# Six edits to a four-layer image kernel: folds moved, small stores from another queue, held pieces spread, a power on POOL, planes in row pairs, two rows swapped

## The chip, the cores and the metric

The kernel runs on one core of one Trainium2 chip. The metric is the device time of one execution in microseconds (us), from the first to the last instruction, as the median of several executions. Engines are called as the profile calls them: PE (TensorE), DVE (VectorE), ACT (ScalarE), POOL (GpSimd) and SP (SyncE); PEld is PE loading weights.

## The reference

The input is an image of 256 by 256 tokens with 128 channels in fp32. Four layers follow one another, each with a group norm in front and a residual around it. Shortened:

```python
x = x + attention(gn(x))      # layer norm, row attention with 4 heads, gate
x = x + gated_product(gn(x))  # a, b = sigmoid((x@W1+b1)*(x@W2+b2)); z = einsum('bikc,bkjc->bijc', a, b), 16 channels
                              # out = sigmoid(x@Wg+bg) * (layernorm(z) @ Wz + bz)
x = x + normalised_product(gn(x))
x = x + shifted_conv(gn(x))   # a 9-tap convolution to one channel, shifts, two 1x1 products

def normalised_product(z):    # 128 channels
    zn = (z - mean(z)) * rsqrt(var(z) + 1e-5)       # over the channels, for each token
    a = sigmoid(zn @ Wga + bga) * (zn @ Wla + bla)
    b = sigmoid(zn @ Wgb + bgb) * (zn @ Wlb + blb)
    k = einsum('bimc,bmjc->bijc', a, b)             # 128 products of 256x256 planes
    return sigmoid(zn @ Wgo + bgo) * (layernorm(k) @ Wlo + blo)
```

The factor `rsqrt(var(z) + 1e-5)` is one number per token, 65536 in all.

## The kernel before

Channels lie on the 128 partitions, tokens along the columns. A *piece* is 2048 tokens (1 MB), and there are 32. The kernel is a chain of passes over the pieces; between two passes everything waits for a statistic or for data that the pass before has stored. In order: load, transpose and statistics; variance of the first layer norm; attention; gate projections; 16 plane products and their normalisation; gated update of x; normalised projections; 128 plane products; output pass; tap sums and image; last pass.

The normalised projections make the factor once in four pieces, in one tile of 128x512 (16 of its 128 rows are live). When the block's turn comes, its rows are spread over the partitions by matmuls and multiplied in:

```python
        def sums5(b):                 # after the second piece of a block of four: the sums for the next block
            ...                       # 32 matmuls into st: mean and mean square
            nc.scalar.activation(mean2, st[:, 0, :], AF.Square, bias=off2)
            nc.vector.tensor_tensor(var, st[:, 1, :], mean2, ALU.subtract)
            nc.vector.tensor_scalar(var, var, 0.0, None, ALU.max)
            nc.scalar.activation(var, var, AF.Sqrt, bias=epst)
            nc.vector.reciprocal(rs2[b], var)

        def normalise5(s):
            rb = broadcast_rows(psX, rs2[s // KB], s, "p5_rb")     # 4 matmuls
            ...                       # zn = (x - mean) * rb on DVE
```

Small results, 32 rows of four times 512 tokens per piece, go to memory by one store from ACT's queue, in the gate projections and in the tap sums:

```python
    def store_groups(dst, s, src):
        nc.scalar.dma_start(dst[:, s * SC : (s + 1) * SC].rearrange("c (q t) -> q c t", q=4), src)
```

A product of two planes reads rows p and p + 128 into partition p, so each packet is one row of 256 numbers, 1 KB (by the packet records of before, 95697 packets of 1024 bytes from 2684 to 2999 us):

```python
            A = sb.tile([P, 8, N], F32, name="p6_A")
            nc.sync.dma_start(A, aD[4 * q : 4 * q + 4, :].rearrange("c (t p n) -> p (c t) n", p=P, n=N))
```

Of the kernel before, what the change touches and what calls it, by code (L numbers as in the profile page):

```python
# [8 lines left out]
F32 = mybir.dt.float32  # L9
AF = mybir.ActivationFunctionType  # L10
# [20 lines left out]
def kernel(ctx: ExitStack, tc: tile.TileContext, a: dict, out: bass.AP):  # L31
# [104 lines left out]
    def store_groups(dst, s, src):  # L136

        nc.scalar.dma_start(dst[:, s * SC : (s + 1) * SC].rearrange("c (q t) -> q c t", q=4), src)
# [48 lines left out]
    with tc.tile_pool(name="f0", bufs=1) as sb, tc.tile_pool(name="f0ps", bufs=1, space=PSUM) as ps:  # L187
        cen = sb.tile([P, P], F32, name="f0_c")
        nc.vector.tensor_scalar(cen, ident, -1.0 / D, None, ALU.add)
        wa = sb.tile([P, 4 * D + NH], F32, name="f0_a")  # L190
        nc.vector.tensor_scalar(wa, w0, ln_w, None, ALU.mult)
        wb = sb.tile([P, 4 * D + NH], F32, name="f0_b")
        nc.vector.tensor_scalar(wb, w0, ln_b, None, ALU.mult)
        for lo, hi in ((0, 4 * D), (4 * D, 4 * D + NH)):
            pc = ps.tile([P, hi - lo], F32, name="f0_pc", tag=f"f0_pc{lo}")
            nc.tensor.matmul(pc, lhsT=cen, rhs=wa[:, lo:hi], start=True, stop=True)
            nc.vector.tensor_copy(w0c[:, lo:hi], pc)
        pq = ps.tile([P, 3], F32, name="f0_pq")
        for j, i in enumerate((0, 1, 3)):
            nc.tensor.matmul(pq[:, j : j + 1], lhsT=w0[:, i * D : (i + 1) * D], rhs=ln_b, start=True, stop=True)  # L200
        nc.vector.tensor_copy(cqkg, pq)
        pv = ps.tile([P, D], F32, name="f0_pv")
        nc.tensor.matmul(pv, lhsT=ones, rhs=wb[:, 2 * D : 3 * D], start=True, stop=True)
        for k in range(4):
            nc.vector.tensor_copy(cv[:, k, :], pv)

        w2c_ = const.tile([P, 6, D], F32, name="w2c_")
        wa2 = sb.tile([P, 6, D], F32, name="f0_a2")
        nc.vector.tensor_scalar(wa2[:, 0:5, :], w2[:, 0:5, :], lniw, None, ALU.mult)
        nc.vector.tensor_scalar(wa2[:, 5, :], w2[:, 5, :], lnow, None, ALU.mult)  # L210
        for lo, hi in ((0, 4), (4, 6)):
            pc = ps.tile([P, (hi - lo) * D], F32, name="f0_pc2", tag=f"f0_pc2{lo}")
            nc.tensor.matmul(
                pc, lhsT=cen, rhs=wa2[:, lo:hi, :].rearrange("p w d -> p (w d)"), start=True, stop=True
            )
            nc.vector.tensor_copy(w2c_[:, lo:hi, :].rearrange("p w d -> p (w d)"), pc)
        pb2 = ps.tile([P, 6], F32, name="f0_pb2")
        for i in range(6):
            nc.tensor.matmul(
                pb2[:, i : i + 1], lhsT=w2[:, i, :], rhs=lnib if i < 5 else lnob, start=True, stop=True  # L220
            )
        nc.vector.tensor_tensor(b2w, b2w, pb2, ALU.add)
        pt_ = ps.tile([P, NH], F32, name="f0_pt")
        nc.tensor.matmul(pt_, lhsT=ones, rhs=wb[:, 4 * D :], start=True, stop=True)
        nc.vector.tensor_copy(ctri, pt_)

    RES = NSC // 2 + 2
    with tc.tile_pool(name="x0", bufs=1) as xres, tc.tile_pool(name="p0", bufs=3) as sb:
        held = {s: xres.tile([P, SC], F32, name=f"x0_{s}") for s in range(RES, NSC)}
        with tc.tile_pool(name="p0ps", bufs=6, space=PSUM) as ps:  # L230
            for s in range(NSC):
# [12 lines left out]
                if s not in held:  # L244
                    nc.sync.dma_start(xT[:, s * SC : (s + 1) * SC], xc)

# [409 lines left out]
    with tc.tile_pool(name="x1", bufs=1) as xres, tc.tile_pool(name="xs1", bufs=3) as xsb:  # L656
        held = {s: xres.tile([P, SC], F32, name=f"x1_{s}") for s in range(R1)}
        with tc.tile_pool(name="p3", bufs=3) as sb, tc.tile_pool(name="p3ps", bufs=3, space=PSUM) as ps:
            for s in range(NSC):
# [15 lines left out]
                nc.scalar.activation(ab, s1, AF.Sigmoid)  # L675
                store_groups(abD, s, ab)


        order = sorted(range(NSC), key=lambda s: (s + 0.5) / R1 if s < R1 else (s - R1 + 0.4) / (NSC - R1))
        loaded = {}  # L680

# [653 lines left out]
```

## Time and profile before

Before: 4266.16 us, median of 3 runs (4259.32 to 4276.3), clock 0.879. The passes in the trace of before, each counted from one characteristic instruction to the next:

| stretch | us |
|---|---|
| start to the attention's first product | 341.4 |
| attention, to the first sigmoid of the gate projections | 1254.9 |
| gate projections and 16 plane products, to the last store of the normalised z issued | 224.9 |
| gated update, to the first sums of the normalised projections | 266.3 |
| normalised projections, to the first plane product | 596.1 |
| 128 plane products, to the first row broadcast of the output pass | 326.4 |
| output pass, to the first tap sum | 384.1 |
| tap sums and image, to the last pass's first fetch of the image | 210.7 |
| last pass | 661.3 |

The page's busy line, and its chain that ended last (followed back from the last instruction, by engine, then by line):

```profile
PE 3274.0 (77%) x20256; PEld 1706.4 (40%) x20256; DVE 2567.3 (60%) x2581; ACT 1965.5 (46%) x2290; POOL 1769.1 (41%) x752
...
PE 28%; DMA 8%; POOL 5%; DVE 4%; issue 3%; ACT 1%; POOLq 0%; SPq 0%; DVEq 0%; ACTq 0%
```

No engine is busy all the time, and the followed chain names PE for only 28%. POOL, with 5%, is seldom what others wait for.

### The profile page before, as it was taken

The numbers are of one execution on the slowest core, as the hardware profiler recorded it, in microseconds if no ns is written. First come the engines' busy times: TensorE is split into PE (matmuls) and PEld (weight loads), VectorE is DVE, ScalarE is ACT, GpSimd is POOL, SyncE is SP. The second block draws the span as 40 slices with busy tenths as digits, with TensorE's granted clock in tenths as the row PEclk, the third lists the DMA queues.
The fourth block names the chain that finished last, engine by engine and source line by source line (L and its number), as shares of the span: only waits on it lengthen the run. The fifth ranks groups of instructions, "written<-read, shape, count | busy, mean of one in ns | idle before, by whom it ended". The sixth has DMA issues, their size and how long they took to land. (4 is left out here: it accounts for less than half of the span.)

```text
span 4266.2 us, 52074 instructions
## 1 busy us (share of the span) xinstructions
PE 3274.0 (77%) x20256; PEld 1706.4 (40%) x20256; DVE 2567.3 (60%) x2581; ACT 1965.5 (46%) x2290; POOL 1769.1 (41%) x752
## 2 busy tenths in 40 slices
PE   3568999999999975567799999899788631555555
PEld 3414555555555531322233333777333200333333
DVE  3526888888888861256544444455566422777775
ACT  2555777777777742222334343344455410333332
POOL 3005777777777740345300000455334200555554
PEclk8788999999999987777899999999899855777777
DMA  6882333333333337477645343999777575444543
GB/s 240 304 305 85 116 111 116 116 110 116 115 111 116 115 130 265 174 242 241 237 161 193 150 182 123 310 311 315 281 287 282 207 247 191 156 164 165 164 164 92
DMA packets 320535, 800.54 MB, mean 188 GB/s; under 512 B 21311, under 2 KB 205132, under 8 KB 265756
## 3 DMA queue, kind: packets, MB, share of 16 engines
q1 hardware_dynamic: 243756, 745.87, 49.5%
q10 hardware_dynamic: 74496, 50.33, 3.8%
q8 instruction: 162, 2.65, 0.3%
q0 software_dynamic: 2032, 0.95, 0.1%
q14 instruction: 89, 0.73, 0.0%
HBM read 503.47 MB, written 293.60 MB: 187 GB/s over the span
## 5 line engine op out<-in xcount | busy, mean ns | idle before, releaser
L459 DVE TENSOR_TENSOR p_e<-p_S,triT 128x1024 f32<-128x1024 f32 x512 | 609.4, 1212 | 144.9 <-PE p_S L449 144.9
L469 POOL TENSOR_TENSOR p_es<-p_e 128x1024 f32<-128x1024 f32 x256 | 603.2, 2367 | 124.0 <-issue 67.3
L467 ACT ACTIVATE p_e<-p_e,mbT 128x1024 f32<-128x1024 f32 x512 | 551.8, 1137 | 61.4 <-DVE p_e L459 59.7
L873 PE MATMUL p_pm<-p_zn,wf 128*128 128x512 f32 x1024 | 464.7, 610 | 22.0 <-ACT p_a L894 20.6
L434 PE MATMUL p_mm<-p_xn,wf 128*128 128x512 f32 x768 | 407.1, 614 | 8.1 <-POOL p_xn L407 8.1
L407 POOL TENSOR_TENSOR p_xn<-p_xn,p_rs 128x1024 f32<-128x1024 f32 x64 | 153.6, 2400 | 492.5 <-DMA p_rs<-rsD 299.8
L1153 PE MATMUL p_pt<-ident,p_v 128*128 128x128 f32 x512 | 116.3, 421 | 282.7 <-POOL p_v L1146 282.7
L1127 POOL TENSOR_TENSOR p_z<-p_z,p_e 128x2048 f32<-128x2048 f32 x32 | 144.3, 4509 | 437.0 <-DMA p_e<-imgD 232.1
L873 PEld LDWEIGHTS p_pm<-p_zn,wf 128*128 128x128 f32 x1024 | 188.8, 194 | 296.3 <-issue 193.4
L449 PE MATMUL p_S<-p_q,p_k 32*128 32x256 f32 x4096 | 296.1, 401 | 5.0 <-DVE p_e L459 5.0
L1133 PE MATMUL p_pm<-p_z,w2c 128*128 128x512 f32 x512 | 246.6, 637 | 64.9 <-POOL p_z L1127 61.8
L449 PEld LDWEIGHTS p_S<-p_q,p_k 32*128 32x128 f32 x4096 | 186.1, 184 | 161.6 <-PE p_mm L425 91.7
L918 POOL MEMSET p_k<- 128x512 f32 x1 | 0.5, 524 | 602.0 <-DMA bD<-p_b 602.0
L482 PE MATMUL p_o<-p_e,p_v 128*32 128x256 f32 x4096 | 247.6, 382 | 0.0
L1293 PE MATMUL tp_z<-p_B,tp_at 128*128 128x256 f32 x1024 | 232.0, 384 | 18.1 <-DMA p_B<-bD 17.9
L1007 POOL TENSOR_TENSOR p_x<-p_x,p_g 128x2048 f32<-128x2048 f32 x32 | 145.1, 4534 | 234.9 <-DVE p_g L1004 202.2
L1146 POOL TENSOR_TENSOR p_v<-p_v,p_x 128x2048 f32<-128x2048 f32 x32 | 196.7, 6147 | 97.6 <-DVE p_v L1144 78.5
L931 POOL TENSOR_TENSOR p_k<-p_k,p_sq 128x512 f32<-128x512 f32 x128 | 162.5, 1270 | 159.2 <-ACT p_sq L929 159.2
L1153 PEld LDWEIGHTS p_pt<-ident,p_v 128*128 128x128 f32 x512 | 104.2, 226 | 309.2 <-POOL p_v L1146 309.2
L1293 PEld LDWEIGHTS tp_z<-p_B,tp_at 128*128 128x128 f32 x1024 | 193.1, 191 | 49.6 <-DMA p_B<-bD 22.7
L1142 DVE TENSOR_TENSOR p_v<-p_r,p_z 128x2024 f32<-128x2024 f32 x32 | 153.9, 4810 | 64.8 <-ACT p_r L1134 64.8
L1157 ACT COPY p_o<-p_pt 128x512 f32<-128x512 f32 x64 | 37.5, 586 | 332.1 <-PE p_pt L1153 332.1
(318 smaller groups left out, 6205.0 us busy)
## 6 DMA issues: line engine op xcount, KB each, us to landing
p_x<-x2T SPq DMA_DIRECT2D x64, 1024.0 KB
p_x<-x1T SPq DMA_DIRECT2D x48, 1024.0 KB
p_x<-x3T SPq DMA_DIRECT2D x31, 1152.0 KB
p_x<-x3T SPq DMA_DIRECT2D x33, 1024.0 KB
p_x<-in_x_dram SPq DMA_DIRECT2D x32, 1024.0 KB
p_x<-xT SPq DMA_DIRECT2D x64, 512.0 KB
p_rs<-rsD SPq DMA_DIRECT2D x64, 512.0 KB
p_rb<-rzD SPq DMA_DIRECT2D x256, 128.0 KB
```

Source lines behind the costliest of these rows:

```text
L434: nc.tensor.matmul(pm, lhsT=w, rhs=t["xn"][:, cs_], start=True, stop=True)
L449: nc.tensor.matmul(Ss[h // 2][:, h % 2, u, :], lhsT=t["k"][hp, r * N + u * P : r * N + (u + 1) * P], rhs=t["q"][hp, r * N : (r + 1) * N], ...
L459: nc.vector.tensor_tensor(e[:, :, 2 * p : 2 * p + 2, :].rearrange("p u h n -> p h u n"), Ss[p], triT[:, 2 * p : 2 * p + 2, :, :], ALU.add,)
L467: nc.scalar.activation(e[:, u, :, :], e[:, u, :, :], AF.Exp, bias=mbT[:, u, i : i + 1])
L469: nc.gpsimd.tensor_tensor(es, e[:, 0, :, :], e[:, 1, :, :], ALU.add)
L482: nc.tensor.matmul(t["o"][hp, r % 2, :], lhsT=t["v"][:, r * 2 + u, hp], rhs=e[:, u, h, :], start=(u == 0), stop=(u == 1),)
L873: nc.tensor.matmul(pm[:, c, :], lhsT=wf2[:, i, :], rhs=zns[s][:, k * CK : (k + 1) * CK], start=True, stop=True)
L931: nc.gpsimd.tensor_tensor(k2, k2, sq, ALU.add)
L1133: nc.tensor.matmul(pm, lhsT=w2c, rhs=src[:, 2 * c : 2 * c + 2, :], start=True, stop=True)
L1146: nc.gpsimd.tensor_tensor(q, q, xt[:, 1:, :], ALU.add)
L1153: nc.tensor.transpose(pt[:, k, :], qf[:, b * P : (b + 1) * P], ident)
L1293: nc.tensor.matmul(pz[:, t, :], lhsT=at[:, u, t * P : (t + 1) * P], rhs=B[:, 2 * c + u, :], start=(u == 0), stop=(u == 1))
```

## The change

Its intent: take small costs out of eight stretches. The core of the diff, cut:

```diff
 # 1. folds of the layer norms' weights: moved from in front of the first pass to behind its statistics
 # 2. small stores: the queue is an argument, and both callers give nc.gpsimd
-        nc.scalar.dma_start(dst[:, s * SC : (s + 1) * SC].rearrange("c (q t) -> q c t", q=4), src)
+        queue.dma_start(dst[:, s * SC : (s + 1) * SC].rearrange("c (q t) -> q c t", q=4), src)
 # 3. every fourth piece held between the gate projections and the gated update; zn fetched two blocks ahead
-        held = {s: xres.tile([P, SC], F32, name=f"x1_{s}") for s in range(R1)}
+        held = {s: xres.tile([P, SC], F32, name=f"x1_{s}") for s in range(0, NSC, NSC // R1)}
-            for i, s in enumerate(order):
+            for s in range(NSC):
 # 4. the factor as a power on POOL
-            nc.vector.tensor_scalar(var, var, 0.0, None, ALU.max)
-            nc.scalar.activation(var, var, AF.Sqrt, bias=epst)
-            nc.vector.reciprocal(rs2[b], var)
+            nc.vector.tensor_scalar(var, var, 0.0, EPS, ALU.max, ALU.add)
+            nc.gpsimd.tensor_tensor(rs2[b], var, mhalf.to_broadcast([P, CK]), ALU.pow)
 # 5. planes in row pairs: partition p holds rows 2p and 2p+1, packets of 2 KB; the transposes read every second column
-            nc.sync.dma_start(A, aD[4 * q : 4 * q + 4, :].rearrange("c (t p n) -> p (c t) n", p=P, n=N))
+            nc.sync.dma_start(A, aD[4 * q : 4 * q + 4, :].rearrange("c (p t) -> p c t", p=P))
+    Ac = A[:, c, :].rearrange("p (t k u) -> p t u k", t=2, u=2)
-            nc.tensor.transpose(pa[:, u, t * P : (t + 1) * P], A[:, 2 * c + t, u * P : (u + 1) * P], ident)
+            nc.tensor.transpose(pa[:, u, t * P : (t + 1) * P], Ac[:, t, u, :], ident)
 # 6. output pass: the next piece's z rows before its k rows
-                    (normalise_z if h else normalise_k)(s + 1)
+                    (normalise_k if h else normalise_z)(s + 1)
 ... (the same layouts for B, K, zn and the factor of k; order and buffers of the gated update)
```

More of the change, by code (lines that the diff above doesn't have):

```diff
@@ L134, with store_groups @@
     b2 = column("L3_conv_b2")
-    def store_groups(dst, s, src):
-        nc.scalar.dma_start(dst[:, s * SC : (s + 1) * SC].rearrange("c (q t) -> q c t", q=4), src)
+    def store_groups(queue, dst, s, src):
+        queue.dma_start(dst[:, s * SC : (s + 1) * SC].rearrange("c (q t) -> q c t", q=4), src)
     def gn_finish(stats, name):
@@ L186 @@
     nc.vector.memset(slide[:, 31:32], 1.0 / D)
-    with tc.tile_pool(name="f0", bufs=1) as sb, tc.tile_pool(name="f0ps", bufs=1, space=PSUM) as ps:
-        cen = sb.tile([P, P], F32, name="f0_c")
-        nc.vector.tensor_scalar(cen, ident, -1.0 / D, None, ALU.add)
-        wa = sb.tile([P, 4 * D + NH], F32, name="f0_a")
-        nc.vector.tensor_scalar(wa, w0, ln_w, None, ALU.mult)
-        wb = sb.tile([P, 4 * D + NH], F32, name="f0_b")
-        nc.vector.tensor_scalar(wb, w0, ln_b, None, ALU.mult)
-        for lo, hi in ((0, 4 * D), (4 * D, 4 * D + NH)):
-            pc = ps.tile([P, hi - lo], F32, name="f0_pc", tag=f"f0_pc{lo}")
-            nc.tensor.matmul(pc, lhsT=cen, rhs=wa[:, lo:hi], start=True, stop=True)
-            nc.vector.tensor_copy(w0c[:, lo:hi], pc)
-        pq = ps.tile([P, 3], F32, name="f0_pq")
-        for j, i in enumerate((0, 1, 3)):
-            nc.tensor.matmul(pq[:, j : j + 1], lhsT=w0[:, i * D : (i + 1) * D], rhs=ln_b, start=True, stop=True)
-        nc.vector.tensor_copy(cqkg, pq)
-        pv = ps.tile([P, D], F32, name="f0_pv")
-        nc.tensor.matmul(pv, lhsT=ones, rhs=wb[:, 2 * D : 3 * D], start=True, stop=True)
-        for k in range(4):
-            nc.vector.tensor_copy(cv[:, k, :], pv)
-        w2c_ = const.tile([P, 6, D], F32, name="w2c_")
-        wa2 = sb.tile([P, 6, D], F32, name="f0_a2")
-        nc.vector.tensor_scalar(wa2[:, 0:5, :], w2[:, 0:5, :], lniw, None, ALU.mult)
-        nc.vector.tensor_scalar(wa2[:, 5, :], w2[:, 5, :], lnow, None, ALU.mult)
-        for lo, hi in ((0, 4), (4, 6)):
-            pc = ps.tile([P, (hi - lo) * D], F32, name="f0_pc2", tag=f"f0_pc2{lo}")
-            nc.tensor.matmul(
-                pc, lhsT=cen, rhs=wa2[:, lo:hi, :].rearrange("p w d -> p (w d)"), start=True, stop=True
-            )
-            nc.vector.tensor_copy(w2c_[:, lo:hi, :].rearrange("p w d -> p (w d)"), pc)
-        pb2 = ps.tile([P, 6], F32, name="f0_pb2")
-        for i in range(6):
-            nc.tensor.matmul(
-                pb2[:, i : i + 1], lhsT=w2[:, i, :], rhs=lnib if i < 5 else lnob, start=True, stop=True
-            )
-        nc.vector.tensor_tensor(b2w, b2w, pb2, ALU.add)
-        pt_ = ps.tile([P, NH], F32, name="f0_pt")
-        nc.tensor.matmul(pt_, lhsT=ones, rhs=wb[:, 4 * D :], start=True, stop=True)
-        nc.vector.tensor_copy(ctri, pt_)
     RES = NSC // 2 + 2
@@ L245 @@
                     nc.sync.dma_start(xT[:, s * SC : (s + 1) * SC], xc)
+        with tc.tile_pool(name="f0", bufs=1) as fsb, tc.tile_pool(name="f0ps", bufs=1, space=PSUM) as ps:
+            cen = fsb.tile([P, P], F32, name="f0_c")
+            nc.vector.tensor_scalar(cen, ident, -1.0 / D, None, ALU.add)
+            wa = fsb.tile([P, 4 * D + NH], F32, name="f0_a")
+            nc.vector.tensor_scalar(wa, w0, ln_w, None, ALU.mult)
+            wb = fsb.tile([P, 4 * D + NH], F32, name="f0_b")
+            nc.vector.tensor_scalar(wb, w0, ln_b, None, ALU.mult)
+            for lo, hi in ((0, 4 * D), (4 * D, 4 * D + NH)):
+                pc = ps.tile([P, hi - lo], F32, name="f0_pc", tag=f"f0_pc{lo}")
+                nc.tensor.matmul(pc, lhsT=cen, rhs=wa[:, lo:hi], start=True, stop=True)
+                nc.vector.tensor_copy(w0c[:, lo:hi], pc)
+            pq = ps.tile([P, 3], F32, name="f0_pq")
+            for j, i in enumerate((0, 1, 3)):
+                nc.tensor.matmul(pq[:, j : j + 1], lhsT=w0[:, i * D : (i + 1) * D], rhs=ln_b, start=True, stop=True)
+            nc.vector.tensor_copy(cqkg, pq)
+            pv = ps.tile([P, D], F32, name="f0_pv")
+            nc.tensor.matmul(pv, lhsT=ones, rhs=wb[:, 2 * D : 3 * D], start=True, stop=True)
+            for k in range(4):
+                nc.vector.tensor_copy(cv[:, k, :], pv)
+            w2c_ = const.tile([P, 6, D], F32, name="w2c_")
+            wa2 = fsb.tile([P, 6, D], F32, name="f0_a2")
+            nc.vector.tensor_scalar(wa2[:, 0:5, :], w2[:, 0:5, :], lniw, None, ALU.mult)
+            nc.vector.tensor_scalar(wa2[:, 5, :], w2[:, 5, :], lnow, None, ALU.mult)
+            for lo, hi in ((0, 4), (4, 6)):
+                pc = ps.tile([P, (hi - lo) * D], F32, name="f0_pc2", tag=f"f0_pc2{lo}")
+                nc.tensor.matmul(
+                    pc, lhsT=cen, rhs=wa2[:, lo:hi, :].rearrange("p w d -> p (w d)"), start=True, stop=True
+                )
+                nc.vector.tensor_copy(w2c_[:, lo:hi, :].rearrange("p w d -> p (w d)"), pc)
+            pb2 = ps.tile([P, 6], F32, name="f0_pb2")
+            for i in range(6):
+                nc.tensor.matmul(
+                    pb2[:, i : i + 1], lhsT=w2[:, i, :], rhs=lnib if i < 5 else lnob, start=True, stop=True
+                )
+            nc.vector.tensor_tensor(b2w, b2w, pb2, ALU.add)
+            pt_ = ps.tile([P, NH], F32, name="f0_pt")
+            nc.tensor.matmul(pt_, lhsT=ones, rhs=wb[:, 4 * D :], start=True, stop=True)
+            nc.vector.tensor_copy(ctri, pt_)
@@ L675 @@
                 nc.scalar.activation(ab, s1, AF.Sigmoid)
-                store_groups(abD, s, ab)
-        order = sorted(range(NSC), key=lambda s: (s + 0.5) / R1 if s < R1 else (s - R1 + 0.4) / (NSC - R1))
+                store_groups(nc.gpsimd, abD, s, ab)
         loaded = {}
         def fetch1(pool, tag, bufs):
-            for s in order:
+            for s in range(NSC):
                 if s not in held and s not in loaded:
@@ L697 @@
             for q in range(4):
-                A = sb.tile([P, 8, N], F32, name="z_A")
-                nc.sync.dma_start(A, abD[4 * q : 4 * q + 4, :].rearrange("c (t p n) -> p (c t) n", p=P, n=N))
-                B = sb.tile([P, 8, N], F32, name="z_B")
-                nc.sync.dma_start(B, abD[16 + 4 * q : 20 + 4 * q, :].rearrange("c (t p n) -> p (c t) n", p=P, n=N))
+                A = sb.tile([P, 4, 2 * N], F32, name="z_A")
+                nc.sync.dma_start(A, abD[4 * q : 4 * q + 4, :].rearrange("c (p t) -> p c t", p=P))
+                B = sb.tile([P, 4, 2 * N], F32, name="z_B")
+                nc.sync.dma_start(B, abD[16 + 4 * q : 20 + 4 * q, :].rearrange("c (p t) -> p c t", p=P))
                 for c in range(4):
@@ L729 @@
                 nc.sync.dma_start(
-                    znD[4 * q : 4 * q + 4, :].rearrange("c (t p n) -> p (c t) n", p=P, n=N),
-                    zq.rearrange("p c (t n) -> p (c t) n", t=2),
+                    znD[4 * q : 4 * q + 4, :].rearrange("c (p t) -> p c t", p=P),
+                    zq,
                 )
@@ L739, in fetch_zn @@
             def fetch_zn(b):
-                zns[b] = sb.tile([P, 4, CK], F32, name="p4_zn", bufs=4)
+                zns[b] = sb.tile([P, 4, CK], F32, name="p4_zn", bufs=3)
                 for c in range(4):
@@ L745, in fetch_zn, with finish @@
                     )
-            def finish(i, x2):
-                s = order[i]
+            def finish(s, x2):
                 for c in range(4):
@@ L753 @@
             pending = []
+            for b in range(2):
+                fetch_zn(b)
             for _ in range(4):
                 fetch1(sb, "xs2", 4)
-            for i, s in enumerate(order):
-                for b in (s // 4, order[min(i + 2, NSC - 1)] // 4):
-                    if b not in zns:
-                        fetch_zn(b)
+            for s in range(NSC):
+                if s % 4 == 1 and s // 4 + 2 < NSC // 4:
+                    fetch_zn(s // 4 + 2)
                 xt = held[s] if s in held else loaded[s]
@@ L783 @@
                 nc.gpsimd.tensor_tensor(xt, xt, gt, ALU.add)
-                pending.append((i, xt))
+                pending.append((s, xt))
                 if len(pending) > 1:
                     finish(*pending.pop(0))
-                    if order[i - 1] not in held:
+                    if s - 1 not in held:
                         fetch1(*((xsb, "xs", 3) if len(loaded) % 7 < 3 else (sb, "xs2", 4)))
@@ L825 @@
     KB = 4
+    mhalf = const.tile([P, 1], F32, name="mhalf")
+    nc.vector.memset(mhalf, -0.5)
     rs2 = [rs2_pool.tile([P, CK], F32, name=f"rs2_{b}") for b in range(NSC // KB)]
@@ L919 @@
         for q in range(D // 4):
-            A = sb.tile([P, 8, N], F32, name="p6_A")
-            nc.sync.dma_start(A, aD[4 * q : 4 * q + 4, :].rearrange("c (t p n) -> p (c t) n", p=P, n=N))
-            B = sb.tile([P, 8, N], F32, name="p6_B")
-            nc.sync.dma_start(B, bD[4 * q : 4 * q + 4, :].rearrange("c (t p n) -> p (c t) n", p=P, n=N))
-            K = sb.tile([P, 8, N], F32, name="p6_K")
+            A = sb.tile([P, 4, 2 * N], F32, name="p6_A")
+            nc.sync.dma_start(A, aD[4 * q : 4 * q + 4, :].rearrange("c (p t) -> p c t", p=P))
+            B = sb.tile([P, 4, 2 * N], F32, name="p6_B")
+            nc.sync.dma_start(B, bD[4 * q : 4 * q + 4, :].rearrange("c (p t) -> p c t", p=P))
+            K = sb.tile([P, 4, 2 * N], F32, name="p6_K")
             for c in range(4):
                 pz = tri_product(nc, ps, sb, A, B, c, ident, nc.vector.tensor_copy).rearrange("p t n -> p (t n)")
-                nc.scalar.copy(K[:, 2 * c : 2 * c + 2, :].rearrange("p t n -> p (t n)"), pz)
+                nc.scalar.copy(K[:, c, :], pz)
                 sq = sb.tile([P, 2 * N], F32, name="p6_sq")
@@ L931 @@
                 nc.gpsimd.tensor_tensor(k2, k2, sq, ALU.add)
-            nc.sync.dma_start(kD[4 * q : 4 * q + 4, :].rearrange("c (t p n) -> p (c t) n", p=P, n=N), K)
+            nc.sync.dma_start(kD[4 * q : 4 * q + 4, :].rearrange("c (p t) -> p c t", p=P), K)
         nc.vector.scalar_tensor_tensor(k1, k1, -1.0 / D, k1, ALU.mult, ALU.mult)
@@ L939 @@
         nc.sync.dma_start(
-            rkD.rearrange("o (t p n) -> p (o t) n", p=P, n=N), k1.rearrange("p (t n) -> p t n", n=N)
+            rkD.rearrange("o (p t) -> p (o t)", p=P), k1
         )
@@ L1037 @@
             nc.scalar.copy(st, pp)
-            store_groups(sD, s, st)
+            store_groups(nc.gpsimd, sD, s, st)
     with tc.tile_pool(name="img", bufs=1) as sb, tc.tile_pool(name="imgps", bufs=1, space=PSUM) as ps:
@@ L1282, in tri_product @@
 def tri_product(nc, ps, sb, A, B, c, ident, evacuate):
+    Ac = A[:, c, :].rearrange("p (t k u) -> p t u k", t=2, u=2)
+    Bc = B[:, c, :].rearrange("p (u n) -> p u n", u=2)
     pa = ps.tile([P, 2, N], F32, name="tp_a")
@@ L1293, in tri_product @@
             nc.tensor.matmul(
-                pz[:, t, :], lhsT=at[:, u, t * P : (t + 1) * P], rhs=B[:, 2 * c + u, :], start=(u == 0), stop=(u == 1)
+                pz[:, t, :], lhsT=at[:, u, t * P : (t + 1) * P], rhs=Bc[:, u, :], start=(u == 0), stop=(u == 1)
             )
```

## The prediction

> **What bounds the kernel now.** No single engine does: the page shows PE busy 77% of the span, DVE 60%, ACT 46%, POOL 41%. The kernel is a chain of some ten passes over the image, each ended by statistics, so I took it pass by pass. First the busy times by stretch, for five passes in turn: the two gate projections (1595 to 1755 us), the gated update of x (1845 to 2078), the 128 products of planes (2684 to 2999), one period of the output pass, the tap sums (3390 to 3557).
>
> ```profile
> core 0: us, PE busy (x) PEld busy (x) DVE busy (x) ACT busy (x) POOL busy (x), PEclk, DMA share, GB/s
> ...
> 3111.54:3122.64 11.10, 9.44 (x32) 3.50 (x33) 7.21 (x7) 6.30 (x7) 4.54 (x2) 1.00 0.75 284
> 1595.00:1755.00 160.00, 76.82 (x500) 16.74 (x492) 24.03 (x32) 42.11 (x64) 0.00 (x0) 0.73 0.67 252
> 1845.00:2078.00 233.00, 182.98 (x501) 68.83 (x500) 154.41 (x192) 67.98 (x62) 144.79 (x32) 0.83 0.74 234
> 3390.00:3557.00 167.00, 61.58 (x258) 7.04 (x258) 43.07 (x32) 18.73 (x32) 0.00 (x0) 0.51 0.69 248
> 2684.00:2999.00 315.00, 292.17 (x1536) 251.09 (x1535) 169.49 (x256) 139.33 (x257) 161.56 (x128) 0.99 0.99 312
> ```
>
> The products are at the DMA limit (share 0.99). The gate projections and tap sums have every engine under half busy and a DMA share near 0.68: something else paces them. Then the waits of the tap sums, the gated update and the output pass, one line from each answer (total us, times, longest):
>
> ```profile
> ACT p_st L1037 <- DMA sD<-p_st: 135.7, 29, 8.1
> ```
> ```profile
> PE p_pz L774 <- DMA p_zn<-znD: 74.2, 6, 35.8
> ```
> ```profile
> PE p_pm L982 <- DVE p_zn L976: 51.4, 31, 1.7
> ```
>
> The first is a wait for small stores, the second for a fetch that comes late, the third one wait of 1.66 us in each of 31 periods. Then the chain of waits in the normalised projections, where the factor is made once in four pieces:
>
> ```profile
> 2209.84 7.05 PE p_st L848 x64
> ...
> 2216.97 0.70 ACT p_m L854
> ...
> 2220.21 0.72 ACT p_var L858
> ...
> 2220.95 1.28 ACT L894
> ...
> 2222.25 1.12 ACT p_a L894
> ...
> 2223.41 5.23 PE p_pm L873 x8
> ```
>
> PE stands 2.94 us because ACT loads the square-root table, takes the root and loads the sigmoid table back; then it runs eight matmuls in 5.23 us instead of 3.70. Last the start: the first transposes begin only here, though the first piece had landed at 6.6 us by the landing records.
>
> ```profile
> 40.67 7.51 PEld L240 LDWEIGHTS p_t<-ident,p_x 128*128 128x128 f32 x48 [0.47 <-issue]
> ```
>
> [...] The small stores are written as [4, 32, 512] from 128 partitions[...]
>
> ```profile
> q10 hardware_dynamic: 74496, 50.33, 3.8%
> ```
>
> ACT's queue holds 32 output stores of 2048 packets and 64 small stores of 128: 73728. The remaining 768 are completions, and 32 x 16 + 64 x 4 is just 768.
> [...] The first zn fetches (16 partitions each) moved 104 GB/s from 1840 to 1850. [...]
> [...]
> [...]
>
> **The change, part by part.**
>
> *Folds behind the statistics.* The transposes can start at about 7 us instead of 40.7. The three preloaded pieces had landed by 14.6 us and DMA then idled until 45, so about 30 us of loading time is won, not 34, because this pass runs at a DMA share of 0.94 to 0.99. The folds' PE and DVE work (15 to 20 us and 36 to 40 us on the trace, 9 us together) moves onto the path between the last statistic and the factor; part overlaps the 3.6 us aggregate, so +8. I add +4 for folds' DVE operations that the scheduler may put early, where DVE then waits for weights that land at 14 to 37 us. Net -18.
>
> *Small stores from POOL's queue.* Per piece a busy engine carries 8 load packets of 8 KB (0.36 us in these passes) and, if one of the four, 32 store packets of 2 KB at 0.084 us: 2.9 + 2.7 = 5.6 us by estimate; the measured pieces take 163/32 = 5.1 us and 167/32 = 5.2 us. [...] Saved: 32 x 1.2 = 38, of which I book 36 for the gate projections; 32 x 1.3 = 42 [...] for the tap sums. Together -74.
>
> *Every fourth piece held.* Now pieces 0 to 7 are held and used throughout, so two of four zn buffers are pinned and each next block is fetched when it is needed: 74 us of PE wait, 36 of them before the first product and 38 later. With blocks in order and a fetch two blocks ahead the later ones vanish. What remains is DMA: per piece 224 packets of 8 KB x 0.39 / 16 = 5.5 and 64 zn packets x 0.225 / 16 = 0.9, 6.4 us x 32 = 203. The first zn fetch goes ahead of four loads of x, some 9 us earlier. From 1836 to about 2040 instead of 2078: -38, and I add -4 because packets should be shorter than 0.39 us without the bursts.
>
> *POOL power.* A period of four pieces takes 71.9 us: four pieces of 15.0, the sums 7.05, and 4.85 of gap. Without the root, its two tables and the 3.35 us reciprocal nearly all of the gap goes: 7 x 4.5 = -31. The power has some 20 us until its rows are used, except in block 0, where it is on the path: +6 if it takes 10 us (my guess). Net -25.
>
> *Planes in row pairs.* 96 MB in packets of 1 KB (0.052 us by the packet records) become 2 KB ones; the first pass shows 0.094 us for those. 49152 x 0.094 / 16 = 289 us against 319. PE alone needs 2.22 us per plane (6.67 per three when nothing waits), 285 us. So this goes from 320 to about 295: -25; the 16 planes of the gated layer give 1 more.
>
> *z before k in the output pass.* The next piece's z rows are ready half a piece sooner, and k has one more product's time. The 1.66 us wait goes: 11.1 to 9.5, checked against DMA (three transfers of 1 MB a piece are 384 packets of 8 KB: 384 x 0.345 / 16 = 8.3 us). 31 x 1.55 = 48; ACT's 4.4 us of moments may now delay a sigmoid, so I book -40.
>
> Sum: -18 - 74 - 42 - 25 - 26 - 40 = -225. The attention pass (1114 us and more) and the last pass (654 us) are untouched. 4266 - 225 = 4041, put at 4040.
>
> **Rivals.** (a) The power is slow. If POOL takes more than about 20 us for 128x512, PE waits in every block: at 40 us, 7 x 20 for the blocks and 30 more for block 0 are +170, so about 4210 in all. Nothing in the trace measures it; the long slack speaks against it, the missing figure for it. (b) The strided transposes load weights slower: 512 of 0.14 us, doubled +72 us, part hidden: near 4090. (c) The loads do not use what the stores set free: three buffers and a latency of some 8 us give 3.9 us per piece only if both overlap; if the pace stays at 4.5, 64 x 0.6 = +38: 4078. (d) Early-placed fold operations stall DVE until 37 us; the first part becomes +8: 4066. (e) Where DMA is freed, [...] packets lengthen; over the three DMA-heavy passes perhaps +30.
>
> **Range and chances.** The parts are mostly independent; an error of 10 to 15 us in each of six gives about 35. For 8 in 10: 3980 to 4115. Only (a) or two others together would spoil the 2% (85 us): faster 0.93, within 0.05, slower 0.02.
>
> **What would show it.** First transpose near 7 us; pieces of the gate projections and tap sums under 4.2 us; no wait for zn after the first; no table loads inside the normalised projections and a period near 67.3; the products at 2.3 us per plane with packets of 2 KB; periods of 9.5 us in the output pass. Wrong would be: pieces still at 5 us (then the four engines were not the limit), a wait for the power, transposes over 0.3 us, or the output pass waiting for DVE at another product.

- "The four" are DMA engines, as I read the records, which name none. In the trace of before a small store has 4 completions and an output store 16. While small stores moved data, at most four of their packets were under way in 90% of the time in the gate projections and 92% in the tap sums; of the output stores there were 12 or more in 93% of it.
- For the small stores, 1.2 and 1.3 us are the measured 5.1 and 5.2 us a piece less 3.9 us. The 3.9 was an estimate with nothing in the trace for how POOL's queue would spread the stores.
- For the tap sums 38 of the 42 us were booked; the 4 us taken off stood for an effect. So small stores come to -36 - 38 = -74, and the sum, with this term in it, to -225: 4266 - 225 = 4041, put at 4040. Without it, it would be -229.
- In rival (c), the latency of a load in the tap sums of before is 7.6 us (median of 32, from issue to first use).

## The result, and the profile after

After: 4576.12 us, median of 4 runs (4571.91 to 4585.05), against 4270.35 us for before beside it. The ratio is 1.0722, with a 95% interval of 1.0693 to 1.0751: 7% slower, where 5% faster was predicted.

The page after, with the lines that answer to those shown of before:

```profile
PE 3246.8 (71%) x20256; PEld 1710.5 (37%) x20256; DVE 2550.4 (56%) x2574; ACT 1937.9 (42%) x2268; POOL 2478.9 (54%) x824
...
PE 25%; POOL 19%; DMA 6%; DVE 3%; issue 2%; ACT 1%; POOLq 0%; SPq 0%; DVEq 0%; ACTq 0%
...
L858 POOL TENSOR_TENSOR rs<-p_var,mhalf 128x512 f32<-128x512 f32 x8 | 655.4, 81924 | 370.0 <-DVE p_var L857 370.0
```

POOL is busy 710 us longer than before, and its share of the chain rose from 5% to 19%. The last line gives most of it: the eight powers take 81,924 ns each, 655.4 us together. The line of waits shows who paid (total us, times, longest):

```profile
PE p_rb L814 <- POOL rs L858: 518.6, 8, 84.2
```

Eight waits, one per block. One period of the normalised projections, from the chain that ended last (start, length, what):

```profile
2119.92 7.05 PE p_st L848 x64
...
2126.99 0.70 ACT p_m L854
...
2129.02 81.94 POOL rs L858
...
2211.00 2.09 PE p_rb L814 x8
2213.09 14.70 PE p_pm L872 x32
```

(The profile counts two records for each of these matmul calls: x64 is 32 calls, x8 is 4.) As in the chain before, the sums take 7.05 us, and the table loads are gone as intended (15 of 1.28 us each in this pass before, one after). But the power then holds the chain for 82 us. PE still had products of the block before, whose last one ends at 2149.0 in the timeline, and then stood still until 2211.0: 62 us of the power's 82, so a slack of 20.

Now the other passes. The first transpose starts here (timeline, start and length):

```profile
6.28 3.28 PEld L200 LDWEIGHTS p_t<-ident,p_x 128*128 128x128 f32 x16 [6.28 <-issue]
```

And the busy times by stretch for the same five passes as in the prediction: gate projections, gated update, tap sums, plane products, one period of the output pass.

```profile
core 0: us, PE busy (x) PEld busy (x) DVE busy (x) ACT busy (x) POOL busy (x), PEclk, DMA share, GB/s
1570.00:1660.00 90.00, 59.56 (x468) 15.88 (x460) 22.47 (x30) 36.79 (x58) 18.75 (x28) 0.92 1.00 378
1770.00:1960.00 190.00, 158.85 (x456) 58.62 (x448) 137.70 (x172) 62.02 (x57) 129.84 (x29) 0.88 0.79 239
3735.00:3850.00 115.00, 54.89 (x232) 6.44 (x224) 38.85 (x29) 17.01 (x29) 26.70 (x30) 0.51 0.94 327
3096.00:3370.00 274.00, 262.52 (x1384) 232.67 (x1384) 152.80 (x232) 124.47 (x230) 147.00 (x116) 1.00 0.96 326
3425.34:3434.70 9.36, 9.36 (x33) 3.50 (x32) 7.14 (x8) 6.19 (x6) 4.55 (x1) 1.00 0.90 338
```

The gate projections and the tap sums now run at a DMA share of 1.00 and 0.94, where it was 0.67 and 0.69: their pacing limit is gone. The output pass has PE busy in the whole period. The same stretches as in the table of before, side by side:

| stretch | before | after | difference |
|---|---|---|---|
| start | 341.4 | 312.7 | -28.7 |
| attention | 1254.9 | 1255.6 | +0.7 |
| gate projections, 16 products | 224.9 | 175.6 | -49.3 |
| gated update | 266.3 | 244.6 | -21.7 |
| normalised projections | 596.1 | 1091.1 | +495.0 |
| 128 products | 326.4 | 318.3 | -8.1 |
| output pass | 384.1 | 331.8 | -52.3 |
| tap sums, image | 210.7 | 175.2 | -35.5 |
| last pass | 661.3 | 670.0 | +8.7 |
| sum | 4266.2 | 4575.0 | +308.8 |

Of the signs that the prediction named, the first transpose (6.3 us), the paces, the missing table loads, the waits for zn and the output pass came as said. The products came to 2.36 us a plane (274 us for 116) and not 2.3, the period near 67.3 us did not come, and a wait for the power is on its list of what would be wrong.

So the traces say that five of the edits together save 196 us, one costs 495, and the last pass, which no edit touches, is 9 us longer. My theory is that the power's duration, and nothing around it, is the loss. The rivals: POOL's place is the trouble (any work there, or the stores on its queue, delay others); the power has a large start-up and would be cheap in another shape; or the loss needs two of the edits together.

### The profile page after: what moved, and what is told of

Same layout as the page of the kernel before. It is cut to its first block, busy times and chain, and to the rows that moved or that the text cites. A ratio compares the mean times of both kernels' runs of the same rounds, so it can differ in the third digit from the quotient of the medians.

```text
span 4575.0 us, 52129 instructions
## 1 busy us (share of the span) xinstructions
PE 3246.8 (71%) x20256; PEld 1710.5 (37%) x20256; DVE 2550.4 (56%) x2574; ACT 1937.9 (42%) x2268; POOL 2478.9 (54%) x824
## 3 DMA queue, kind: packets, MB, share of 16 engines
q0 software_dynamic: 19440, 17.83, 1.4%
## 4 chain that ended last, share of the span: by engine, by line
PE 25%; POOL 19%; DMA 6%; DVE 3%; issue 2%; ACT 1%; POOLq 0%; SPq 0%; DVEq 0%; ACTq 0%
POOL rs L858 14%; PE p_pm L872 7%; PE p_pm L981 5%; POOL p_v L1145 4%; PE tp_z L1294 3%; PE p_pm L1132 3%; PE p_pt L1152 3%; DMA p_B<-bD 2%; DVE p_v L1141 2%; PE p_st L848 1%; DMA p_x<-x3T 1%; DMA sD<-p_st 1%; PE tp_a L1288 1%; PE p_rz L814 1%; PE p_rb L814 1%
## 5 line engine op out<-in xcount | busy, mean ns | idle before, releaser
L858 POOL TENSOR_TENSOR rs<-p_var,mhalf 128x512 f32<-128x512 f32 x8 | 655.4, 81924 | 370.0 <-DVE p_var L857 370.0
L814 PE MATMUL p_rb<-rs,sel 32*128 32x512 f32 x256 | 44.1, 763 | 518.6 <-POOL rs L858 518.6
L865 DVE SCALAR_TENSOR_TENSOR p_zn<-p_x,gn_mean,p_rb 128x1024 f32<-128x1024 f32 x64 | 78.9, 1274 | 523.9 <-PE p_rb L814 523.9
L893 ACT ACTIVATE p_a<-p_pm,b2w 128x1024 f32<-128x1024 f32 x64 | 71.3, 1114 | 660.4 <-PE p_pm L872 660.4
```

Of the source, the lines that this page charges most:

```text
L858: nc.gpsimd.tensor_tensor(rs2[b], var, mhalf.to_broadcast([P, CK]), ALU.pow)
```

## The experiments

Twelve kernels ran, in three groups; each group shared its runs of before (medians 4267.06, 4265.91 and 4265.99 us).

**The power undone.** All other edits stay.

```diff
-            nc.vector.tensor_scalar(var, var, 0.0, EPS, ALU.max, ALU.add)
-            nc.gpsimd.tensor_tensor(rs2[b], var, mhalf.to_broadcast([P, CK]), ALU.pow)
+            nc.vector.tensor_scalar(var, var, 0.0, None, ALU.max)
+            nc.scalar.activation(var, var, AF.Sqrt, bias=epst)
+            nc.vector.reciprocal(rs2[b], var)
```

> The kernel after with only the factor of the normalised projections taken as before (square root on ACT, reciprocal on DVE); everything else of the change stays. My theory: the power on POOL is the whole reason for the loss. Between the starts of the normalised projections and of the plane products the trace has 596.1 us before and 1091.1 after, 495 more, and no other edit falls into that stretch; so this kernel should take 4576 - 495 = 4081 us, range 4060 to 4100, that is 0.956 of the kernel before, and the eight waits of PE for the factor should be gone. Rival: POOL's stores, or the other order of things, also cost time that the power hides; then it stays above 4120. Second rival: the gains of the other parts came only because something else was late; then it is near 4266.

Measured: 4082.36 us (4077.06 to 4089.21, 5 runs), ratio 0.9573 [0.956, 0.9586]. The normalised projections take 597.9 us, as before. Undoing the power alone gives back 494 us.

**The power alone.** The kernel before with that one edit.

> The kernel before with the power on POOL as its only change. Theory (the power costs the same with or without the other edits, since none of them falls into its stretch): the normalised projections grow by 495 us as in the kernel after, 4267 + 495 = 4762, range 4735 to 4785, ratio 1.116. Rival (the loss needs another edit beside it, such as the stores on POOL's queue): clearly less than 4700.

Measured: 4763.34 us (4759.68 to 4765.91, 4 runs), ratio 1.1167 [1.1149, 1.1184]. The loss, 497 us, is the same without the other edits, so it needs no partner.

**The power on half of the columns** (wrong result: the other half is only copied).

```diff
-            nc.gpsimd.tensor_tensor(rs2[b], var, mhalf.to_broadcast([P, CK]), ALU.pow)
+            hc = CK // 2
+            nc.gpsimd.tensor_tensor(rs2[b][:, :hc], var[:, :hc], mhalf.to_broadcast([P, hc]), ALU.pow)
+            nc.gpsimd.tensor_copy(rs2[b][:, hc:], var[:, hc:])
```

> The kernel after with the power on half of the columns (256 of 512) and a copy for the others: wrong result on purpose, to read the cost law. Theory (cost per column of 128 values, 81.9 / 512 = 0.16 us, and a slack of 20 us): one power takes 41 us, PE waits 21 us in seven blocks and 41 in block 0, 188 us in all instead of 516; total 4576 - 328 = 4248, range 4225 to 4275. Rival (most of the 82 us is fixed, a start-up of the operation): over 4400. Rival (the copy or the wrong values change other stages): the difference does not lie in the normalised projections.

Measured: 4254.53 us (4252.37 to 4257.83, 4 runs), ratio 0.9973 [0.9958, 0.9988]. One power took 41.1 us, and the line of PE's wait for the factor is now this (block 0 is left out of the window):

```profile
PE p_rb L814 <- POOL rs L860: 151.2, 7, 21.6
```

That is 151.2 / 7 = 21.6 us per block, which is the power's 41.1 us less about 20 us of slack. The law "wait = duration less slack" holds at two points.

**The power by itself.** Ten POOL operations behind the last pass, on squared weights.

```diff
+        for i, (pp, n) in enumerate(((128, 512), (128, 256), (128, 128), (128, 64), (128, 16), (16, 512), (64, 512))):
+            r = sb.tile([P, CK], F32, name=f"m_r{i}")
+            nc.gpsimd.tensor_tensor(r[:pp, :n], v[:pp, :n], mhalf[:pp].to_broadcast([pp, n]), ALU.pow)
+        ...  # exponent 2; base 1 everywhere; a plain product
```

> The cost of the power by itself: the kernel with Newton's method in place of the power, with ten POOL operations added behind the last pass: powers of 128x512, 128x256, 128x128, 128x64, 128x16, 64x512 and 16x512 with exponent -0.5, 128x512 with exponent 2, 128x512 with base 1 everywhere, and a product of 128x512. Theory (per column and side by side over the partitions): 82, 41, 20.5, 10.2, 2.6 us for the first five; the same 82 us for 64 and 16 partitions; 82 us whatever base and exponent; 1.3 us for the product. Rival: a fixed part, then 128x16 takes far more than 2.6 us; rival: time goes with the number of values, then 16x512 takes about 10 us; rival: it depends on the values, then exponent 2 or base 1 is short. The total says nothing here, since the operations stand at the end.

Measured (one run, correct); from the groups by form, with busy us and mean ns:

```profile
L1183 POOL TENSOR_TENSOR m_one<-ones,mhalf 128x512 f32<-128x512 f32 x1 | 82.4, 82400 | 9.6 <-DMA out_dram<-p_o 9.6
L1179 POOL TENSOR_TENSOR m_r<-m_v,mhalf 128x512 f32<-128x512 f32 x1 | 81.9, 81918 | 0.0
L1179 POOL TENSOR_TENSOR m_r<-m_v,mhalf 16x512 f32<-16x512 f32 x1 | 81.9, 81915 | 0.0
...
L1181 POOL TENSOR_TENSOR m_sq<-m_v,m_two 128x512 f32<-128x512 f32 x1 | 81.9, 81905 | 0.0
...
L1179 POOL TENSOR_TENSOR m_r<-m_v,mhalf 128x16 f32<-128x16 f32 x1 | 2.9, 2885 | 0.0
L1185 POOL TENSOR_TENSOR m_mul<-m_v 128x512 f32<-128x512 f32 x1 | 1.0, 1029 | 0.0
```

From 16 to 512 columns it is (81,918 - 2,885) / 496 = 159 ns a column, with a fixed part of about 0.3 us. It does not matter how many partitions are used (16, 64 or 128), and the two exponents and the two sets of bases that were tried make no difference beyond 0.5 us. The product of the same tile with itself takes 1.03 us, one eightieth.

**The same factor from plain POOL operations.** One DVE operation on the bits gives a first guess, and three rounds of Newton's method follow.

```diff
-            nc.gpsimd.tensor_tensor(rs2[b], var, mhalf.to_broadcast([P, CK]), ALU.pow)
+            y = rs2[b]
+            t = sb.tile([P, CK], F32, name="p5_t", bufs=1)
+            nc.vector.tensor_scalar(y.bitcast(I32), var.bitcast(I32), -0.5, 1597463007.0, ALU.mult, ALU.add)
+            for _ in range(3):
+                nc.gpsimd.tensor_tensor(t, y, y, ALU.mult)
+                nc.gpsimd.tensor_tensor(t, t, var, ALU.mult)
+                nc.gpsimd.tensor_scalar(t, t, -0.5, 1.5, ALU.mult, ALU.add)
+                nc.gpsimd.tensor_tensor(y, y, t, ALU.mult)
```

> The kernel after with the power written as twelve plain POOL operations: one DVE operation on the bit pattern gives a first guess of the inverse root, then three rounds of Newton's method of three products and one scale-and-add each. From the trace POOL takes 1.27 us for a product of 128x512, so 9 x 1.27 + 3 x about 0.8 = 14 us, inside the slack of 20 us that PE had between the start of the power (2129.0) and its last product before the wait (2149.0). Theory (it is the time of this operation and not its place on POOL that costs): no wait for the factor in blocks 1 to 7, a period of 131.05 - 62.05 = 69.0 us, block 0 pays 14 us instead of 82; 7 x 62.05 + 68 = 502 us less than 4576, so 4074, range 4050 to 4095. Rival (POOL's work of whatever kind stands in the way of DVE here, or its semaphores come late): waits of PE for POOL remain, and it stays above 4120.

Measured: correct, 4062.4 us (4055.08 to 4064.61, 5 runs), ratio 0.9516 [0.9503, 0.9529]. One round, and the use of the factor, in the timeline:

```profile
2130.32 1.04 POOL L865 TENSOR_TENSOR p_t<-rs 128x512 f32<-128x512 f32 x1 [53.74 <-DVE rs L861]
2131.43 1.27 POOL L866 TENSOR_TENSOR p_t<-p_t,p_var 128x512 f32<-128x512 f32 x1
2132.79 0.62 POOL L867 TENSOR_SCALAR p_t<-p_t 128x512 f32<-128x512 f32 x1
2133.50 1.27 POOL L868 TENSOR_TENSOR rs<-rs,p_t 128x512 f32<-128x512 f32 x1
```

The twelve operations end at 2143.8, and PE takes the factor at 2149.6 without a wait; in the whole stretch PE waits for POOL once, 16.2 us in block 0. The period is 67.2 us, against 72.1 with the root on ACT and about 131 with the power. So POOL was a good place, and the idea of the edit (no table loads, work in the slack) was worth its gain; only the operation was wrong.

**The same on DVE, spread.** Nine operations, two behind each product's evacuation.

```diff
+            for _ in range(3):
+                todo.append(lambda: nc.vector.scalar_tensor_tensor(t, y, -0.5, y, ALU.mult, ALU.mult))
+                todo.append(lambda: nc.vector.tensor_tensor(t, t, var, ALU.mult))
+                todo.append(lambda: nc.vector.scalar_tensor_tensor(y, t, 1.5, y, ALU.add, ALU.mult))
 ...
+                    root5(2)         # takes two from the list, behind each gated product
```

> The kernel after with Newton's method on DVE instead of POOL, three operations a round, put two at a time behind the products' evacuations in the slack. Theory: nothing of the nine operations (about 0.6 us each by the DVE rows of that size) is on PE's path in blocks 1 to 7, so the period stays at 67.2 as with POOL's version, and block 0 pays 6 us instead of 13: 4062 - 7 = 4055, range 4042 to 4068. Rival (DVE[...] frees the PSUM tiles later): the period grows by 1 us or more, and it is slower than POOL's version, 4065 to 4090.

Measured: correct, 4055.73 us (4043.67 to 4059.32, 5 runs), ratio 0.9496 [0.948, 0.9512]. It is the fastest kernel, by the medians 5% faster than before and 11% faster than after. The period stays at 67.4 us, and the normalised projections take 567.7 us instead of 575.3. The intervals of the two Newton kernels overlap a little and they ran in different groups, so the order of the two totals is not certain; that both beat the kernel before and the kernel after is.

**The other edits, one by one.** These start from the kernel with the power undone (4082.36 us), and each takes back a part of the change.

*Small stores from ACT again, one per piece.*

```diff
-                store_groups(nc.gpsimd, abD, s, ab)
+                store_groups(nc.scalar, abD, s, ab)
 ... (the same in the tap sums)
```

> The kernel with the square root back (4082 us), with the small stores as in the kernel before (one from ACT each). Theory: this undoes exactly what the traces show for those two passes, 49 us and 36 us: 4082 + 85 = 4167, range 4145 to 4185. Rival (part of the gain is owed to the blocks held in another order, or to the row pairs, which touch the same pass): less than 4140.

Measured: 4163.24 us (4154.76 to 4173.68, 4 runs), 80.9 us more; the two stretches grew from 177.1 to 225.5 and from 174.5 to 208.7.

*Small stores from ACT, four of 32 rows each.*

```diff
-        queue.dma_start(dst[:, s * SC : (s + 1) * SC].rearrange("c (q t) -> q c t", q=4), src)
+        for q in range(4):
+            nc.scalar.dma_start(dst[:, s * SC + q * CK : s * SC + (q + 1) * CK], src[32 * q : 32 * q + 32, :])
```

> The kernel with the square root back (4082 us), its 64 small stores issued from ACT again, but each as four stores of 32 rows, so that the slowest dimension is 32 and not 4. Theory (the stores were slow because they ran on four DMA engines only, not because ACT issued them): the gate projections and the tap sums keep their pace of about 3.1 and 3.9 us a piece, total 4082, range 4070 to 4105 with ACT's additional issues. Rival (ACT as issuer, or its queue, was the limit): back to 4.8 and 5.1 us a piece, 49 + 36 = 85 us more, 4167.

Measured: 4091.4 us (4088.23 to 4102.61, 4 runs). The queue lines of the kernel after (q10 is ACT's, q0 POOL's, which has the small stores there), and below them ACT's in this kernel (packets, MB, share):

```profile
q10 hardware_dynamic: 66048, 33.56, 2.6%
q0 software_dynamic: 19440, 17.83, 1.4%
```
```profile
q10 hardware_dynamic: 78336, 50.35, 4.2%
```

ACT's queue holds 65536 packets of output stores in both. In the kernel after the other 512 are completions, 16 for each of 32 output stores. Here 64 x 128 = 8192 packets of small stores come to it and 78336 - 65536 - 8192 = 4608 completions, which is 16 for each of 32 + 256 stores; in the kernel before a small store had 4, and mostly no more than four of its packets were under way (90 and 92% of the time, as above). The same engine issues, and the speed is back: tap sums 169.1 us (208.7 with 4 completions a store), gate projections 190.7 (225.5). So how narrow a store ran, in my reading the number of its DMA engines, was the limit: of all that was won in the tap sums, and of 34.8 us of the 48.4 won in the gate projections. There 13.6 us are left against POOL's queue (177.1), and for these ACT as the issuer is a candidate: the trace of this kernel has, from 1575 to 1670 us, ten waits of ACT's sigmoids in which ACT waits for nothing but its own issues, which the trace of the kernel with POOL's queue has not. No run tests it.

```profile
ACT p_ab L676 <- issue: 34.4, 10, 4.4
```

How POOL's queue spread its stores is not shown either. It took 17408 packets more than before (19440 against 2032), which is 272 for a store, and its data packets are of 4 KB by the packet records, where ACT's are of 2 KB.

*The two orders undone:* pieces 0 to 7 held again with the late fetch, and k before z in the output pass.

```diff
-                    (normalise_k if h else normalise_z)(s + 1)
+                    (normalise_z if h else normalise_k)(s + 1)
 ... (held, order and fetch_zn of the gated update as in the kernel before)
```

> The kernel with the square root back (4082 us), with two orders undone that lie in different passes: pieces 0 to 7 held again in the gated update (with its interleaved order and the late fetch of zn), and k before z in the output pass. Theory from the traces before and after, each in its own stretch: gated update 244 to 266 us, output pass 332 to 384 us, so 22 + 52 = 74 more, 4156, range 4135 to 4175. Rival: the output pass owes part of its gain to something else (the layout of k, the addresses of the tiles): it stays below 370. Rival for the last pass: if its 8 us extra come from where these tiles lie, it returns to about 661 us.

Measured: 4150.34 us (4145.24 to 4158.63, 4 runs). The gated update went from 243.9 to 266.3 us and the output pass from 331.7 to 383.0. The last pass fell from 669.4 to 663.1.

*Planes in 1 KB packets again* (layouts and `tri_product` as in the kernel before).

> The kernel with the square root back (4082 us), with the planes read and written in packets of 1 KB again. Theory: the products were at the edge of PE and DMA alike, so the row pairs gave only 8 us there and 1 to 2 us in the gated layer's products: 4082 + 10 = 4092, range 4080 to 4105; products 320 to about 327 us. Rival (my prediction's reading, DMA alone was the limit and the pairs gave 25 us): 4107 or more. Rival for the last pass: if k's layout in memory causes its 8 us, it returns to about 661 us.

Measured: 4088.86 us (4085.43 to 4092.34, 4 runs). The products' stretch went from 320.3 to 327.8 us. The intervals of the two totals overlap (ratios 0.9572 to 0.9601 here, 0.956 to 0.9586 with the pairs), so the gain is read from the stretch alone: it is 317.2 to 321.4 us in the ten kernels with the pairs that can be compared, and 326.4 to 327.8 in the three without.

*Contiguous transposes* (wrong result).

```diff
-    Ac = A[:, c, :].rearrange("p (t k u) -> p t u k", t=2, u=2)
+    Ac = A[:, c, :].rearrange("p (t u k) -> p t u k", t=2, u=2)
```

> The kernel with the square root back (4082 us), with the planes' transposes reading contiguous columns instead of every second one: wrong result on purpose, the same count and size of everything. The weight loads of the transposes should fall from 0.207 us to the 0.143 us of the kernel before. Theory (PE is the limit of the products at 2.26 us a plane and these loads lie beside its matmuls): the products stay at 320 us, within 5. Rival (the strided loads are on PE's path and ate what the larger packets gave): 512 x 0.064 = 33 us less, partly taken back by DMA, products at 295 to 305.

Measured: 4079.77 us (4073.07 to 4088.67, 4 runs); the products 320.1 us, against 320.3. The weight loads of the transposes in the kernel after, then here (ns: least, median, most):

```profile
L1288 PEld LDWEIGHTS tp_a<-ident,p_A x512: 194/209/231, 3079.7 to 3378.1; 128*128 128x128 f32 x171
```
```profile
L1289 PEld LDWEIGHTS tp_a<-ident,p_A x512: 137/140/230, 2576.7 to 2876.4; 128*128 128x128 f32 x171
```

A step of two makes a load half as long again (209 ns against 140, medians), and nothing of it reaches the end (320.3 us against 320.1).

*Folds in front again.* The block of folds stands before the first pass, as in the kernel before.

> The kernel with the square root back (4082 us), with the folds in front of the statistics again. Theory: the stretch up to the attention pass's first product returns from 306 to 313 us, as the kernels with the folds behind have it, to 338 to 341 us, so about 29 us more: 4111, range 4095 to 4125. Rival (my prediction: 18 us, since loading is at its limit anyway): 4100. Rival for the last pass: if the 8 us extra come from the place of the folds' constants in SBUF, it returns to about 661 us.

Measured: 4111.02 us (4107.28 to 4120.42, 4 runs), 28.7 us more. The first stretch took 340.3 us.

## Why the prediction was wrong

**The step that failed** is "POOL power", and in it the words "+6 if it takes 10 us (my guess)". The duration was 81.9 us. The rest of that step was right: the slack measured 20 us, the wait was the duration less the slack, and block 0 paid in full. The power's eight waits are 518.6 us; the gap that the edit was to remove was removed as well, which is why the stretch grew by 495 and not by 519. (With Newton's method on POOL the period is 67.2 us, where the prediction has 67.3.) The prediction was off by 536 us (4576 against 4040), and this one term, booked at -25 and measured at +495, is 520 of them.

Rival (a) had the mechanism, and its rule comes close. At 82 us it gives 7 x 62 for the blocks and 72 for block 0, 506 on top of 4040, 4546. It was set aside by "the long slack speaks against it", with a chance of 2% for the slower outcome. That argument was empty, since a slack of 20 us says nothing about a duration nobody has measured. The missing figure was known and written down, and should have widened the range.

**The other parts**, as booked, as the stretches show them, and by experiment (medians against 4082.36 us, or the stretch where two edits were undone together):

| part | booked | trace | experiment |
|---|---|---|---|
| folds | -18 | -28.7 | -28.7 |
| small stores | -74 | -84.8 | -80.9 |
| every fourth piece held | -42 | -21.7 | -22.4 |
| row pairs | -26 | -8.1 | -6.5 |
| z before k | -40 | -52.3 | -51.3 |
| power | -25 | +495.0 | +494 |

Without the power the sum of the bookings is 4266 - 200 = 4066, and the kernel with the root took 4082. The mechanisms held, but for the row pairs, where DMA was not the only limit; the sizes were off in three ways. That the sum came within 16 us is partly luck, since 34 us booked too low and 38 us booked too high nearly cancel.

- *Folds, z before k and gate projections were booked too low.* The last statistic came 30.8 us earlier (164.5 against 195.3), about as worked out, but the 12 us booked against it for the folds on the path and for early DVE work were mostly not there: from the last statistic to the first use of its factor the trace has 4 us more (12.1 against 8.0). The output pass has a period of 9.4 us, where 9.5 was predicted, and the 8 us withheld for ACT were not needed. The gate projections run at 3.1 us a piece (95.5 us from first to last of 32), where 3.9 was booked.
- *Held pieces were booked too high.* The waits for zn fell as predicted, with one left for the first block. But the booking then let the transfers run at a full DMA share, and the trace has 0.79, hardly above the 0.74 of before. The lines of PE's wait and of SP's queue, after:

```profile
PE p_pz L772 <- DMA p_zn<-znD: 26.7, 6, 23.4
```
```profile
SPq L684 <- DMA x2T<-p_x: 152.7, 17, 11.8
```

  SP waits 152.7 us for the stored x2 piece to land before it may load the next x into its buffer. It did so before, too:

```profile
SPq L686 <- DMA x2T<-p_x: 141.5, 17, 11.1
```

  But in the trace of before PE has no wait for x in this pass, and in that of after it has nine, 28.6 us together. So too few free buffers, hidden before behind the waits for zn, seem to be what is left. This is read from the traces; no run has more buffers.
- *Row pairs were booked too high.* I took DMA for the only limit, from its share of 0.99. The packets did become 2 KB, and 49152 of them at 0.096 us over 16 engines are 295 us, about as booked. But PE alone needs 2.26 us a plane (274 us less 11.5 us of waits for transfers, over 116 planes), 290 us, and from first to last the products take 306. Two limits within 2% of each other are not a floor one can book down to. That the strided loads do not fill this gap is shown by the run with contiguous ones; that it is waits of PE on single transfers is argued.

Of the other rivals, (b) came true in the duration of the loads (0.14 to 0.21 us) and not at the end. (c) did not come: the paces were 3.1 and 3.9 us. (d) came true in its wait, but the stretch did not get longer. In the first pass DVE stood 16.4 us, until 37.7, before an operation on weights that the scheduler had put early, and 1.3 and 0.8 us before two more:

```profile
DVE wz L649 <- DMA g<-in_L_conv_ln_g_dram: 16.4, 1, 16.4
```

The DMA share was full (1.01 by the profile) from 20 to 38 us, so loading went on beside this wait, and 0.72 from 38 to 50. No run takes the wait away, so what it costs is not shown. For (e), lengthened packets, I have no clean test; by the packet records the 8 KB packets got shorter in the gate projections (0.328 us against 0.350) and in the tap sums (0.345 against 0.371).

**What stays open.** The last pass is 661 us in the kernel before, 664 in that with the power alone, 668 to 672 in the ten others with the change that can be compared, and 663 with the two orders undone. (The place of the folds and the layout of the planes, suspected above, are not it: 669.6 and 669.8 us with each undone.) So one of those two orders, neither of which lies in this pass, seems to cost 6 to 8 us here; each is one profile, and how it comes about I cannot say.

## What to carry to other kernels

An operation that no trace gives a duration for must be measured alone before it is put on a chain, or the range must cover many times the guess (here it was eight times); "it has slack" is an argument only once both sides have a number. When such an operation turns out slow, the place may still be right: here the same engine, in the same slack, did the job in 13.5 us with twelve plain operations. And a store that ACT issues as four groups of 32 rows, and that shows 4 completions where others show 16, is worth splitting, or giving to POOL's queue: here the first brought 71.8 us back and the second 80.9.
